# Layer 1 edges: kv tiles in two steps, variances on ScalarE, one message product

## Chip, cores and metric

The kernel runs on one core of a Trainium2 chip, as one launch. The metric is the device time of an execution in microseconds (us). Five engines work side by side, each through its own queue in order: TensorE (PE, with its weight loads PEld), VectorE (DVE), ScalarE (ACT), GpSimd (POOL) and SyncE (SP).

## The reference

Two layers of a graph network over 3125 nodes with 256 features and 50000 edges, all in float32. Each layer adds a message-passing part, a mixing part and a feed-forward part to the node rows. The change lies in layer 1, where the first two are:

```python
h_fwd, h_rev = h @ W_forward.T, h @ W_reverse.T               # 3125 x 64 each
messages = h_fwd[src] * direction[:, 0:1] + h_rev[src] * direction[:, 1:2]
scores = leaky_relu(einsum('ef,hf->eh', messages, attn), 0.2)  # 4 heads
exp_scores = exp(scores - scores.max(axis=0))
norm = exp_scores / (segment_sum(exp_scores, dst)[dst] + 1e-10)
out_gnn = [segment_sum(messages * norm[:, hd:hd+1], dst) for hd in range(4)]

q, k, v = split(x @ Wqkv.T)                                    # 8 heads of 64
k, v = inst_norm_lastdim(k), inst_norm_lastdim(v)              # (t - mean) / sqrt(var + 1e-5)
out_mix = einsum('nhd,hde->nhe', q, einsum('nhd,nhe->hde', k, v)) / n @ Wout.T + bout
```

The edges come sorted by target node (`dst`). What is called Galerkin in the kernel is the second block.

## The kernel before

The nodes stand in 25 tiles of 128 rows (NT = 25, P = 128). The edges stand in 391 columns of 128 (NJ = 391), one edge per partition, and are taken in 50 groups (SPANS): 4 columns, then 48 groups of 8, then 3. Group i adds into a block of 64 nodes.

`layer1_mix` runs over the groups as a pipeline of three stages; the queues of TensorE, VectorE and ScalarE hold the work in exactly the order in which the loop writes it (a manual schedule). In turn i:

- `fetch` and `request`: POOL issues one indirect DMA (`gather`, L71) per column, 128 rows of 136 floats from the table `tab1` into `g`: both products h_fwd and h_rev of the source node, each with its four scores (W = 68 = 64 + 4). Eight gathers of group i+3 are issued in each turn, in portions of 2, 2, 1, 2 and the rest, each portion behind the latest named VectorE operation. `g` has four buffers.
- `messages(i)`, VectorE: the two directions are copied into PSUM (L1652), two products (L1653 and L1654), their sum (L1655), leaky ReLU on the scores (L1657), maximum over the columns (L1662); TensorE turns the maximum (L1664).
- `weigh(i-1)`, VectorE: weights into PSUM (L1702), messages times the weights of four heads (L1703, 128x2048).
- `maximum(i)`, VectorE: running maximum (L1671 to L1673); TensorE spreads it over the partitions (L1677).
- `products(i-1)`, TensorE: one matmul pair per column, one-hot targets against weighted messages (L1709).
- `add(i-2)`: VectorE rescales and adds into `acc` (L1717, L1718); ScalarE copies (L1719, L1721).
- `ones_of(i)`, VectorE: the one-hot matrix `hot` (L1695).
- `exponents(i)`: ScalarE copies the spread maximum out of PSUM (L1682, `top_b`), VectorE subtracts it (L1683), ScalarE takes two exponentials (L1685, L1687).
- then one step of `galerkin`, in three turns out of four up to turn 34 and in every turn after it.

`galerkin` is a generator; each `next` does one step. Its first step makes the weights `wkv`, with each head's mean taken out, so that a key or value has mean zero and its variance is the mean of squares. Then come 26 steps, one per kv tile and one to finish: the step of tile t first ends tile t-1 (sum of its squares L1797, variance L1798, product of the two variances L1800, root on ScalarE L1801, reciprocal L1803, scaling L1804, four matmuls into `pdots` L1807), and then makes tile t (eight matmuls through `token_matmul`, L276; two copies on ScalarE L1817; one square of the whole tile L1819). After the tiles come ten steps that form the product matrix and add its result to x (L1848, L1862, L1864, L1855). The exponentials and the root are in different activation tables, so ScalarE loads a table between them (shown at L1685 and L1801).

Of the kernel before, what the change touches and what calls it, by code (L numbers as in the profile page):

```python
# [9 lines left out]
F32 = mybir.dt.float32  # L10
# [3 lines left out]
AF = mybir.ActivationFunctionType  # L14
OP = mybir.AluOpType
AX = mybir.AxisListType
# [6 lines left out]
P = 128  # L23
NT = 25
# [41 lines left out]
LN_EPS = 1e-5  # L66
# [64 lines left out]
class Kernel:  # L131
# [1462 lines left out]
    def layer1_mix(self, acc):  # L1594
        nc, tc, a = self.nc, self.tc, self.a
        W, HD = 68, 64
        with ExitStack() as m:
            big = m.enter_context(tc.tile_pool(name="l1", bufs=1))
            wk = m.enter_context(tc.tile_pool(name="l1w", bufs=2))
            gp = m.enter_context(tc.tile_pool(name="l1g", bufs=3))  # L1600
            ps_a = m.enter_context(tc.tile_pool(name="l1pa", bufs=2, space=PSUM))
# [5 lines left out]
            xT, tab1 = self.xT, self.tab1  # L1607
# [13 lines left out]
            sides = own[:, 2 * P + 64:2 * P + 64 + 2 * GROUP].rearrange("p (j i) -> p j i", i=2)  # L1621
# [11 lines left out]
            def fetch(i):  # L1633
                j0, n = SPANS[i]
                g = gp.tile([128, GROUP, 2 * W], F32, name="g1", bufs=4)
                wanted.extend((g[:, k, :], self.t_src[:, j0 + k:j0 + k + 1]) for k in range(n))
                return g

            def request(count, behind=None):

                for out, index in wanted[:count]:
                    ins = gather(nc, out, tab1[:], index)
                    if behind is not None:
                        self.after(ins, behind.ins.name, "turns with the groups")
                        behind = None
                del wanted[:count]

            def messages(i, g):

                j0, n = SPANS[i]  # L1650
                o = gp.tile([128, GROUP, W], F32, name="msg1")
                nc.vector.tensor_copy(sides[:, :n, :], self.t_dir[:, j0:j0 + n, :])  # L1652
                nc.vector.tensor_mul(o[:, :n, :], g[:, :n, :W], sides[:, :n, 0:1].to_broadcast([128, n, W]))  # L1653
                nc.vector.tensor_mul(g[:, :n, W:], g[:, :n, W:], sides[:, :n, 1:2].to_broadcast([128, n, W]))  # L1654
                nc.vector.tensor_add(o[:, :n, :], o[:, :n, :], g[:, :n, W:])  # L1655
                s = gp.tile([128, GROUP, 4], F32, name="score1")
                nc.vector.scalar_tensor_tensor(s[:, :n, :], o[:, :n, HD:], 0.2, o[:, :n, HD:],  # L1657
                                               op0=OP.mult, op1=OP.max)
                if j0 + n == NJ:
                    nc.vector.tensor_scalar(s[:, n - 1, :], s[:, n - 1, :], late, None, op0=OP.add)  # L1660
                mx = gp.tile([128, 4], F32, name="mx1")
                self.latest = nc.vector.tensor_reduce(mx, s[:, :n, :].rearrange("p j h -> p h j"), AX.X, OP.max)  # L1662
                pt = ps_s.tile([4, 128], F32, name="psm")
                nc.tensor.transpose(pt, mx, self.ident)  # L1664
                return o, s, pt
# [24 lines left out]
            def ones_of(i):  # L1690

                j0, n = SPANS[i]
                hot = gp.tile([128, GROUP, P], F32, name="hot")
                iota = own[:, i % 2 * P:i % 2 * P + P]
                self.latest = nc.vector.scalar_tensor_tensor(  # L1695
                    hot[:, :n, :], self.t_dst[:, j0:j0 + n, None].to_broadcast([128, n, P]),
                    float(HALF * (1 - i)), iota[:, None, :].to_broadcast([128, n, P]),
                    op0=OP.add, op1=OP.is_equal)
                return hot

            def weigh(n, o, v):
                nc.vector.tensor_copy(weight[:, :n, :], v[:, :n, :, HD])  # L1702
                self.latest = nc.vector.tensor_mul(v[:, :n, :, :HD], o[:, :n, None, :HD].to_broadcast([128, n, 4, HD]),  # L1703
                                     weight[:, :n, :, None].to_broadcast([128, n, 4, HD]))

            def products(n, v, hot):
                pw = ps_w.tile([P, 4, HD + 1], F32, name="pw")
                for k in range(n):
                    nc.tensor.matmul(pw.rearrange("p h c -> p (h c)"), hot[:, k, :],  # L1709
                                     v[:, k, :, :].rearrange("p h c -> p (h c)"), start=(k == 0), stop=(k == n - 1))  # L1710
                return pw
# [13 lines left out]
            with tc.manual_schedule(engines={ET.PE, ET.DVE, ET.Activation}):  # L1725
                todo = self.galerkin(big, wk, ps_a, ps_c, xT, own[:, 2 * P + 96:2 * P + 104])
                S = len(SPANS)
                ahead = [fetch(i) for i in range(3)]
                request(len(wanted))
                msg, exps, summed = {}, {}, {}  # L1730
                for i in range(S + 2):
                    if i + 3 < S:
                        ahead.append(fetch(i + 3))
                    if i < S:
                        n = SPANS[i][1]
                        o, s, pt = messages(i, ahead[i])
                        request(2, self.latest)
                    if 0 <= i - 1 < S:
                        weigh(SPANS[i - 1][1], msg[i - 1][0], exps[i - 1][2])
                        request(2, self.latest)  # L1740
                    if i < S:
                        pb = maximum(pt)
                    if 0 <= i - 1 < S:
                        summed[i - 1] = products(SPANS[i - 1][1], exps[i - 1][2], msg[i - 1][1])
                    if 0 <= i - 2 < S:
                        add(i - 2, *exps[i - 2][:2], summed[i - 2])
                        request(1, self.latest)
                    if i < S:
                        msg[i] = o, ones_of(i)
                        request(2, self.latest)  # L1750
                        exps[i] = exponents(n, s, pb)
                    if i % 4 != 3 or i > 34:
                        next(todo, None)
                    request(len(wanted), self.latest)
                last = exps[S - 1][0]
                for _ in todo:
                    pass
# [10 lines left out]
    def galerkin(self, big, wk, ps_a, ps_c, xT, scales=None):  # L1768
# [3 lines left out]
        nc, a = self.nc, self.a  # L1772
        wkv = big.tile([128, 2, 1024], F32, name="wkv")
# [18 lines left out]
        kvs = {}  # L1792
        for t in range(NT + 1):
            if t > 0:
                kv, sq = kvs.pop(t - 1)
                var = wk.tile([P, 16], F32, name="kv_var")
                nc.vector.tensor_reduce(var, sq, AX.X, OP.add)  # L1797
                nc.vector.tensor_scalar(var, var, 1.0 / 64, LN_EPS, op0=OP.mult, op1=OP.add)  # L1798
                both = wk.tile([P, 8], F32, name="kv_both")
                nc.vector.tensor_mul(both, var[:, 0:8], var[:, 8:16])  # L1800
                nc.scalar.activation(both, both, AF.Sqrt)  # L1801
                inverse = both if scales is None else scales
                nc.vector.reciprocal(inverse, both)  # L1803
                nc.vector.tensor_mul(kv[:, 8:, :], kv[:, 8:, :], inverse[:, :, None].to_broadcast([P, 8, 64]))  # L1804
                for hp in range(4):
                    p = held(t - 1)
                    nc.tensor.matmul(pc[:, hp, :],  # L1807
                                     kv[:p, 8 + 2 * hp:10 + 2 * hp, :].rearrange("p a b -> p (a b)"),
                                     kv[:p, 2 * hp:2 * hp + 2, :].rearrange("p a b -> p (a b)"),
                                     start=(t == 1 and hp == 0), stop=(t == NT and hp == 3),  # L1810
                                     skip_group_check=True)
            if t < NT:
                kv = wk.tile([P, 16, 64], F32, name="kv")
                for i in range(2):
                    pk = ps_a.tile([P, 512], F32, name="ln_pt")
                    self.token_matmul(pk, xT, t, wkv[:, :, 512 * i:512 * i + 512])
                    nc.scalar.copy(kv[:, 8 * i:8 * i + 8, :].rearrange("p a b -> p (a b)"), pk)  # L1817
                sq = wk.tile([P, 16, 64], F32, name="kv_sq", bufs=1)
                nc.scalar.activation(sq, kv, AF.Square)  # L1819
                kvs[t] = kv, sq  # L1820
            yield
        dots = big.tile([128, 4, 128], F32, name="dots")
        nc.vector.memset(dots, 0.0)
        for s in (slice(0, 64), slice(64, 128)):
# [19 lines left out]
        g = big.tile([128, 2, D], F32, name="gm")  # L1844
# [795 lines left out]
```

## Time and profile before

| what | value |
|---|---|
| median of 3 runs | 2501.61 us (2496.76 to 2501.92) |
| the profiled execution, its time | 2496.96 us |
| its span | 2495.2 us |
| busy over the span: PE, DVE, ACT, POOL | 82%, 59%, 33%, 63% |
| first gather to last matmul of the edge stage | 1463.7 to about 2009 us |
| L1703 (`weigh`), full groups | 2.29 us each |
| L1797 (sum of squares) | 25 x 1.21 us |
| L1819 (squares) | 25 x 1.06 us |
| reciprocal L1803 waiting for the root L1801 | 16.4 us in 25 times |

A line of the timeline gives the start in us, the length in us, the engine, the line of the kernel, the operation, the tile written and the tile read, and shapes as partitions x elements; brackets hold the idle time of the engine just before and what ended it. A line of the table by stage gives, for each stretch, the busy us of each engine with the number of instructions, then the mean granted TensorE clock (1 is full), the DMA share and GB/s.

### The profile page before, as it was taken

To read this page: it belongs to the slowest core of one execution; us is meant where nothing else is said; L and a number is where in the kernel's file an instruction comes from. 1 tells how busy PE (TensorE), PEld (TensorE's weight loads), DVE (VectorE), ACT (ScalarE), POOL (GpSimd) and SP (SyncE) were. 2 spreads that over 40 slices of the span, in tenths; PEclk is the share of its full clock that TensorE was granted. 3 is DMA by queue.
4 is the path that set the end of the run, shared out by engine and by line. 5 is a ranking of instruction groups with operands and counts; after the bars stand their busy time and mean duration, and the time that the engine had idled before them with its cause. 6 is when DMAs were issued, how large, how long until landed. Compare 5 with 4: busy or idle time off the path is not lost.

```text
span 2495.2 us, 27313 instructions
## 1 busy us (share of the span) xinstructions
PE 2052.0 (82%) x8239; PEld 1450.5 (58%) x8239; DVE 1465.5 (59%) x3870; ACT 829.8 (33%) x1804; POOL 1565.4 (63%) x1931
## 2 busy tenths in 40 slices
PE   1666799899879989999999647777778779999955
PEld 0433355445555678888888535545556566667644
DVE  6888858986724793221212448888887872223346
ACT  1453144564412113333333324444430042222314
POOL 5888888885000816766666247777776427777743
PEclk9986799999959999999999869999989859999977
DMA  8612539113000225666666332222222112113242
GB/s 269 217 63 102 219 134 324 68 62 111 7 34 5 102 77 164 201 193 200 198 191 187 116 99 55 56 55 56 55 62 46 38 27 38 28 21 80 57 126 78
DMA packets 191721, 263.31 MB, mean 106 GB/s; under 512 B 57234, under 2 KB 152071, under 8 KB 191563
## 3 DMA queue, kind: packets, MB, share of 16 engines
q1 hardware_dynamic: 137551, 211.02, 25.5%
q0 software_dynamic: 48864, 45.64, 8.8%
q10 hardware_dynamic: 5148, 4.80, 0.7%
q8 instruction: 67, 1.10, 0.2%
q14 instruction: 91, 0.75, 0.1%
HBM read 180.80 MB, written 80.55 MB: 105 GB/s over the span
## 4 chain that ended last, share of the span: by engine, by line
PE 59%; DVE 23%; ACT 5%; DMA 4%; POOL 4%; issue 4%; ACTq 0%; DVEq 0%; SPq 0%; POOLq 0%
PE pb L1163 9%; PE pc L1175 8%; PE pb L594 7%; PE fpy L1958 7%; PE fph L1942 7%; DVE v L1703 3%; PE pc L594 3%; PE pw L1709 2%; PE pb L967 2%; PE pc L980 2%; POOL adj L78 2%; PE pb L638 2%; POOL g L71 1%; PE pc L1439 1%; DVE msg L1653 1%
## 5 line engine op out<-in xcount | busy, mean ns | idle before, releaser
L71 POOL DMA_INDIRECT g<-tab,t_src x391 | 378.3, 968 | 197.4 <-issue 153.2
L78 POOL DMA_INDIRECT adj<-ch_sum,ch_place x391 | 415.3, 1062 | 91.0 <-issue 56.5
L78 POOL DMA_INDIRECT sorted<-src,pos x256 | 245.1, 958 | 141.6 <-DVE pos L1462 62.1
L71 POOL DMA_INDIRECT G<-tabg,g_src x256 | 257.9, 1008 | 78.0 <-DMA G<-tabg,g_src 35.7
L1163 PE MATMUL pb<-xs,w 128*128 128x256 f32 x1024 | 226.4, 379 | 0.8 <-ACT h L1165 0.8
L1175 PE MATMUL pc<-w,h 128*128 128x256 f32 x1024 | 226.1, 379 | 0.0
L1709 PE MATMUL pw<-v,hot 128*128 128x260 f32 x782 | 219.5, 442 | 0.0
L1163 PEld LDWEIGHTS pb<-xs,w 128*128 128x128 f32 x1024 | 194.4, 190 | 27.8 <-ACT h L1165 1.0
L594 PE MATMUL pb<-adj,sup 128*128 128x448 f32 (+1 forms) x484 | 196.5, 551 | 14.3 <-DVE r_tot L1309 13.6
L1175 PEld LDWEIGHTS pc<-w,h 128*128 128x128 f32 x1024 | 192.2, 190 | 24.9
L1165 ACT ACTIVATE h<-pb,b 128x256 f32<-128x256 f32 x256 | 121.2, 473 | 253.6 <-issue 168.1
L1709 PEld LDWEIGHTS pw<-v,hot 128*128 128x128 f32 x782 | 169.1, 222 | 31.3
L1958 PE MATMUL fpy<-fw,fh 128*128 128x256 f32 (+1 forms) x800 | 177.7, 379 | 0.0
L1942 PE MATMUL fph<-xT,fw 128*128 128x512 f32 (+2 forms) x448 | 175.2, 545 | 0.0
L1958 PEld LDWEIGHTS fpy<-fw,fh 128*128 128x128 f32 (+1 forms) x800 | 149.6, 187 | 31.8 <-issue 8.2
L78 POOL DMA_INDIRECT slots<-rows,abi x50 | 54.5, 1090 | 164.6 <-DVE which L1085 154.6
L1421 ACT ACTIVATE s_z<-s_y,s_val 128x128 f16<-128x128 f16 x256 | 112.4, 486 | 121.0 <-issue 108.2
L594 PEld LDWEIGHTS pb<-adj,sup 128*128 128x128 f32 x484 | 90.3, 194 | 91.6 <-issue 85.5
L1133 DVE COPY xs<-pa 128x512 f32<-128x512 f32 x32 | 22.1, 691 | 206.6 <-PE pa L1132 206.6
L1944 ACT ACTIVATE fh<-fph,cols 128x512 f32<-128x512 f32 (+2 forms) x112 | 70.3, 632 | 216.2 <-PE fph L1942 216.2
L1942 PEld LDWEIGHTS fph<-xT,fw 128*128 128x128 f32 x448 | 85.7, 192 | 76.7 <-issue 55.8
L1178 DVE SCALAR_TENSOR_TENSOR yo<-pc,own,bg 128x256 f32<-128x256 f32 x64 | 31.0, 484 | 147.0 <-PE pc L1175 147.0
(575 smaller groups left out, 3820.9 us busy)
## 6 DMA issues: line engine op xcount, KB each, us to landing
adj<-zero SPq DMA_DIRECT2D x25, 1600.0 KB
w<-in_L_ffn_W1p_dram SPq DMA_DIRECT2D x32, 1024.0 KB
w<-in_L_ffn_W2p_dram SPq DMA_DIRECT2D x32, 1024.0 KB
adj<-adj SPq DMA_DIRECT2D x24, 896.0 KB
adj<-adj SPq DMA_DIRECT2D x24, 704.0 KB
slots<-empty SPq DMA_DIRECT2D x1, 8448.0 KB
srow<-slots SPq DMA_DIRECT2D x32, 264.0 KB
adj<-ch_sum,ch_place POOLq DMA_INDIRECT x391
```

What stands on the lines that cost most here:

```text
L71: return nc.gpsimd.indirect_dma_start(out=out, out_offset=None, in_=table, in_offset=bass.IndirectOffsetOnAxis(ap=idx, axis=0))
L78: return nc.gpsimd.indirect_dma_start(out=table, out_offset=bass.IndirectOffsetOnAxis(ap=idx, axis=0), in_=rows, in_offset=None, **kw)
L594: nc.tensor.matmul(pm[:, :w], sup[:, b, k * 128:(k + 1) * 128], mats[b, h][:, c0 - PARTS[h][0]:c0 - PARTS[h][0] + w], start=(b == b0), sto ...
L1163: nc.tensor.matmul(ph, w1[:, k, f * 128:(f + 1) * 128], xs[:, k, :], start=(k == 0), stop=(k == 1))
L1165: ins = nc.scalar.activation(h[:, f, :], ph, AF.Gelu, bias=b1[:, f:f + 1])
L1175: nc.tensor.matmul(py, h[:, f, i * 128:(i + 1) * 128], w2[:, f, :], start=(f == 0), stop=(f == FC - 1))
L1421: nc.scalar.activation(z[:, i, k, :], y, AF.Relu, bias=val[:, k, s], scale=val[:, 2 + k, s])
L1703: self.latest = nc.vector.tensor_mul(v[:, :n, :, :HD], o[:, :n, None, :HD].to_broadcast([128, n, 4, HD]), weight[:, :n, :, None].to_broadc ...
L1709: nc.tensor.matmul(pw.rearrange("p h c -> p (h c)"), hot[:, k, :], v[:, k, :, :].rearrange("p h c -> p (h c)"), start=(k == 0), stop=(k == ...
L1942: nc.tensor.matmul(ph[:, :m], w1[:, k, f * 128:(f + 1) * 128], xT[:, k, t0 * P:t0 * P + m], start=(k == 0), stop=(k == 1))
L1944: note(nc.scalar.activation(hs[:, f, :m], ph[:, :m], AF.Gelu, bias=self.col("L1_ffn_b1", ei * FC + f)), m / 512.0)
L1958: nc.tensor.matmul(py[:p], hs[:, f, i * P:i * P + p], w2[:, f, :], start=(f == 0), stop=(f == FC - 1))
```

## The change

Three things are edited.

1. `messages`: the two products become one operation over `g` in place, with the two directions broadcast over the two halves; the sum reads both halves of `g`.
2. `galerkin`: the variances come from ScalarE. Instead of one square of 128x1024 and a sum on VectorE there are 16 squares of 128x64, each with `accum_out` (scale 0.125, so that the sum of squares is divided by 64). A tile's work is cut into two steps: the first ends the variance of tile t-1 up to the root and makes tile t; the second takes the reciprocal, scales and multiplies into `pdots`. With the first step and the last ten there are now 62.
3. `layer1_mix`: `advance(half)` takes the steps. It is called twice in each turn, between `products` and `add` and after `exponents`, and keeps the number of steps done in proportion to the number of halves, so that the 62 steps are spread over the first 46 turns.

```diff
-                nc.vector.tensor_mul(o[:, :n, :], g[:, :n, :W], sides[:, :n, 0:1].to_broadcast([128, n, W]))
-                nc.vector.tensor_mul(g[:, :n, W:], g[:, :n, W:], sides[:, :n, 1:2].to_broadcast([128, n, W]))
-                nc.vector.tensor_add(o[:, :n, :], o[:, :n, :], g[:, :n, W:])
+                both = g[:, :n, :].rearrange("p j (i w) -> p j i w", i=2)
+                nc.vector.tensor_mul(both, both, sides[:, :n, :, None].to_broadcast([128, n, 2, W]))
+                nc.vector.tensor_add(o[:, :n, :], g[:, :n, :W], g[:, :n, W:])
...
+                done, every = 0, 2 * NT + 12
+
+                def advance(half):
+
+                    nonlocal done
+                    while done * 2 * (S - 4) < half * every:
+                        next(todo, None)
+                        done += 1
...
                         summed[i - 1] = products(SPANS[i - 1][1], exps[i - 1][2], msg[i - 1][1])
+                    advance(2 * i + 1)
                     if 0 <= i - 2 < S:
                         add(i - 2, *exps[i - 2][:2], summed[i - 2])
...
                         exps[i] = exponents(n, s, pb)
-                    if i % 4 != 3 or i > 34:
-                        next(todo, None)
+                    advance(2 * i + 2)
                     request(len(wanted), self.latest)
...
         for t in range(NT + 1):
             if t > 0:
-                kv, sq = kvs.pop(t - 1)
-                var = wk.tile([P, 16], F32, name="kv_var")
-                nc.vector.tensor_reduce(var, sq, AX.X, OP.add)
-                nc.vector.tensor_scalar(var, var, 1.0 / 64, LN_EPS, op0=OP.mult, op1=OP.add)
+                kv, var = kvs.pop(t - 1)
+                nc.vector.tensor_scalar(var, var, LN_EPS, None, op0=OP.add)
                 both = wk.tile([P, 8], F32, name="kv_both")
                 nc.vector.tensor_mul(both, var[:, 0:8], var[:, 8:16])
                 nc.scalar.activation(both, both, AF.Sqrt)
+            if t < NT:
+                nxt = wk.tile([P, 16, 64], F32, name="kv")
+                for i in range(2):
+                    pk = ps_a.tile([P, 512], F32, name="ln_pt")
+                    self.token_matmul(pk, xT, t, wkv[:, :, 512 * i:512 * i + 512])
+                    nc.scalar.copy(nxt[:, 8 * i:8 * i + 8, :].rearrange("p a b -> p (a b)"), pk)
+                sq = wk.tile([P, 64], F32, name="kv_sq", bufs=1)
+                var = wk.tile([P, 16], F32, name="kv_var")
+                for h in range(16):
+                    nc.scalar.activation(sq, nxt[:, h, :], AF.Square, scale=0.125, accum_out=var[:, h:h + 1])
+                kvs[t] = nxt, var
+            yield
+            if t > 0:
                 inverse = both if scales is None else scales
                 nc.vector.reciprocal(inverse, both)
...
                                      skip_group_check=True)
-            if t < NT:
-                kv = wk.tile([P, 16, 64], F32, name="kv")
...
-                sq = wk.tile([P, 16, 64], F32, name="kv_sq", bufs=1)
-                nc.scalar.activation(sq, kv, AF.Square)
-                kvs[t] = kv, sq
-            yield
+                yield
```

More of the change, by code (lines that the diff above doesn't have):

```diff
@@ L1811, in galerkin @@
                                      skip_group_check=True)
-            if t < NT:
-                kv = wk.tile([P, 16, 64], F32, name="kv")
[L1814 to L1817, printed above, removed]
-                sq = wk.tile([P, 16, 64], F32, name="kv_sq", bufs=1)
-                nc.scalar.activation(sq, kv, AF.Square)
-                kvs[t] = kv, sq
-            yield
+                yield
         dots = big.tile([128, 4, 128], F32, name="dots")
```

## The prediction

> **What bounds the kernel now.** I read the page first, then the busy time by stage, then the timeline of the edge stage. The edges of layer 1 run from 1464 to 2010 us. While they carry the kv tiles (to about 1850 us) the stages look like this:
>
> ```profile
> core 0: us, PE busy (x) PEld busy (x) DVE busy (x) ACT busy (x) POOL busy (x), PEclk, DMA share, GB/s
> 1500.00:1600.00 100.00, 75.39 (x294) 51.15 (x295) 87.14 (x174) 44.38 (x90) 76.23 (x79) 0.95 0.25 56
> 1600.00:1700.00 100.00, 75.79 (x288) 51.91 (x287) 89.29 (x177) 40.80 (x86) 75.92 (x80) 0.91 0.25 55
> ```
>
> VectorE is busy 87 to 89%, ScalarE 41 to 44%. POOL's 79 gathers in 100 us, each with 0.30 us of issue before it, also fill their queue (8 x 1.27 = 10.2 us per group). VectorE sets the pace: the starts of `weigh` (L1703) at 1626.45, 1637.97, 1645.90, 1657.10 and 1668.62 are 11.5, 7.9, 11.2 and 11.5 us apart. The 7.9 is the one group in four without a kv step. Four groups take 42.6 us (1602.88 to 1645.90 to 1688.07, halved), so three take 31.95.
>
> Why ScalarE costs nothing now is seen in the timeline of one kv group:
>
> ```profile
> 1613.18 3.60 PE L276 MATMUL ln_pt<-wkv,xT 128*128 128x512 f32 x8
> ...
> 1616.82 0.58 ACT L1817 COPY kv<-ln_pt 128x512 f32<-128x512 f32 x1 [1.13 <-PE ln_pt L276]
> ...
> 1617.43 1.06 ACT L1819 ACTIVATE kv_sq<-kv 128x1024 f32<-128x1024 f32 x1
> ...
> 1618.60 0.37 ACT L1721 COPY acc<-pw 64x260 f32<-64x260 f32 x1
> ...
> 1618.99 0.17 ACT L1682 COPY top_b<-psm 128x8 f32<-128x8 f32 x1
> ...
> 1619.42 0.18 DVE L1683 TENSOR_TENSOR score<-score,top_b 128x32 f32<-128x32 f32 x1
> ```
>
> TensorE makes the kv tile, ScalarE copies it, squares it in 1.06 us, and only then reaches L1682, the copy of the maximum. VectorE needs that copy for L1683, one short subtraction that stands in its queue ahead of the whole next group. Here L1682 ends at 1619.16 and `hot` (L1695, from 1618.29 for 1.21 us) at 1619.50: L1683 waits for nothing, with 0.3 us to spare. **That margin is what the change spends.**
>
> **Part 1, one message product.** L1653 and L1654 (721 and 714 ns, 128x544) become one of 128x1088. Rows at 544 and 2048 elements (721 and 2287 ns) give 1.04 ns an element, so 1.29 us; bounds 0.72 (no dearer than one) and 1.43 (both). With the shorter start interval a group's VectorE work gains 0.06 us; by the bounds it gains 0.6 or loses 0.1, at most 30 us over 50 groups, if VectorE sets the pace.
>
> **Part 2, the variances.** Off VectorE goes L1797 (25 x 1.21 = 30.2 us), and the wait of the reciprocal for the root (16.4 us in all) disappears by the two steps. On ScalarE one square of 1.06 us becomes 16 squares of 64 elements, each with its own accumulator. The nearest row is L825:
>
> ```profile
> 210.62 0.38 ACT L825 ACTIVATE sq<-pb 128x256 f32<-128x256 f32 x1 [0.79 <-PE pb L823]
> 210.90 0.19 ACT L825 ACTIVATION_READ_ACCUMULATOR sq<-pb 128x1 f32 x1
> 211.12 0.38 ACT L825 ACTIVATE sq<-pb 128x256 f32<-128x256 f32 x1
> ```
>
> Each accumulator costs a second instruction, and the pair repeats every 0.50 us. The square itself shrinks from 0.383 to 0.255 us (ACTIVATEs of 48 and 96 elements take 243 and 282 ns), so a pair takes 0.375 and a tile **16 x 0.375 = 6.0 us**. Bounds: 0.29 a pair if the read cost nothing (0.255 + 0.03), 0.45 if nothing overlapped (0.255 + 0.195); 4.6 to 7.2 us. All write one `kv_sq`, so each waits for the one before; dependent pieces of ScalarE follow after 0.03 us (L1817 to L1819), which is in the price.
>
> **Part 3, where the steps stand.** Step k is taken at the first half with h > 1.484 k. Tile t's heavy step A (variance end, root, eight matmuls, two copies, 16 squares) is step 2t, near h = 3t; its light step B (reciprocal, scaling, `pdots`) is step 2t+1, near h = 3t+2. So three groups carry two tiles:
> - X: A in the first half, between `products` and `add`.
> - Y: B in the first half, A in the second.
> - Z: B in the second half, but Y's squares stand on ScalarE before its L1682.
>
> The listing of ScalarE's instructions in the changed kernel shows the same: two groups running have 16 squares between their `grown` and the next L1682, the third has none. Before, A came after the exponents, so TensorE worked on the tile while VectorE made the next group's messages. In X it starts only after this group's products.
>
> **X, walked along the wait.** From L1652 to the end of L1673: 5.98 us on VectorE in the group at 1634.83, now 5.92. Transposition and start of products 0.2. Products (L1709) 3.77. The kv matmuls 3.5 (3.60 less overlap). The second copy 0.6. Squares 6.0. `unit`, `acc` and L1682 0.6. L1683 0.2. Sum **20.8 us**. VectorE's own work in X is about 8.4; the other 12 it stands at L1683, with the next group's messages behind it, and POOL's gathers wait for their turns behind those.
>
> **Y and Z.** Y has only VectorE work: 5.92, B's two operations 0.95, L1717 and L1718 0.92, `hot` 1.14, L1683 0.18, the variance's two 0.4: 9.5. Y's products start 6.1 after its own start; 3.77 to 9.9, `pdots` to 10.85, kv matmuls to 14.35, copy to 14.95, squares to 20.95, L1682 to 21.55, L1683 to 21.75, B of Z to **22.7 us** for Y and Z together.
>
> Three groups: 20.8 + 22.7 = 43.5 us. **The clock** adds to this. A product after a quiet TensorE is slow:
>
> ```profile
> 1687.97 0.27 PE L1664 MATMUL psm<-ident,mx 128*4 128x128 f32 x1 [1.01 <-DVE mx L1662]
> 1690.88 0.36 PE L1677 MATMUL psm<-ident,top 4*128 4x4 f32 x2 [2.64 <-DVE top L1672]
> 1691.16 6.56 PE L1709 MATMUL pw<-v,hot 128*128 128x260 f32 x16
> ...
> 1703.05 3.77 PE L1709 MATMUL pw<-v,hot 128*128 128x260 f32 x16
> ```
>
> The slow ones of three neighbouring cases took 6.49, 5.46 and 6.56 us, 6.2 on average. In X the products come after the same two waits, in Y after TensorE has stood through X's squares (over 6 us): both are slow, and both on the path, 2 x 2.4 = 4.8 us. Three groups: 48.3 us.
>
> The Trainium skill (TensorE: Matmul & The Clock Gate, Part 1: The HAM clock gate) halves the clock only after an idle window of about 3.4 us and gives it back after as much work. The trace goes slow after 1.01 and 2.64 us with a 0.27 us transposition between. By the rule X would stay fast and Y lose about 1.7 us, an estimate, for 2663 us.
>
> **The sum.** 25 tiles are 12.5 rounds of three: 12.5 x (48.3 - 31.95) = **+205 us**. The other pieces I take at nothing. The last ten galerkin steps fall on eight groups, not on eleven; TensorE sets the pace there (11.4 us a group) and does the same matmuls, so what each group gains is gone in the number; from the two sides -8 to +8. Table loads (1.28 us, L1685 and L1801) are as many as before at most: the root's runs while ScalarE waits for the matmuls, the exponent's under 2.7 us of the next messages; without that cover 25 x 1.28 = 32 us. The 391 gathers keep number, queue and order; POOL's 30 us per round hide under 48. SP's load of Wout only moves. The profiled execution took 2496.96 us (span 2495.2), 4.65 under the median of 2501.61; the sum is 2497 + 205 = **2702 us**, and that offset, as wide as the spread of the runs, is left out.
>
> **The rivals.**
> - Clock stays full: 12.5 x (43.5 - 31.95) = +144, 2641 us. For it: X's products follow `pdots` by some 4 us only. Against: the 6.56 row.
> - Accumulators dearer: at 0.45 a pair 1.2 us more per tile, +30, 2732; at 0.5, as L825 with its 256 elements, 2 us more per tile, +50, 2752.
> - Accumulators cheap: 0.29 a pair, -1.4 per tile, -35: 2667, or 2606 with the clock full.
> - It ends faster: ScalarE has 4.9 us more per tile, two tiles in 30.6 us of a POOL-paced round, so its share rises from 44% to about 76%. If the squares fell into ScalarE's idle time and L1682 did not queue behind them, VectorE would need 3 x 7.9 + 2 x 1.35 = 26.4 us per round, POOL's 30.6 (three times 10.2) would bind, and 12.5 x (30.6 - 31.95) = -17 gives 2480. It decides at 0.3 us, the margin of L1682 above; against it, the order of ScalarE's queue.
> - The change does not do what it says, since the even spreading loses to the place of A: part of my forecast. Even with squares at their old 1.06 us, X would need 20.8 - 4.9 = 15.9 against 8.4.
>
> **How the numbers follow.** Forecast (slow products, 0.375 a pair) 55%; full clock 22%; dearer accumulators 12%; cheap ones 6%; the faster case 4%; a balance near nothing 1%. The range reaches from 2606, cheap squares at full clock, to 2765 (0.5 a pair, plus 8 of the tail and 5 of the runs' spread). A measurement tells 0.2% from no change. Faster 0.04, same 0.01, slower 0.95.
>
> **What would show it.** Right: L1683 waiting for ScalarE some 25 times, about 15 us in X and 5 to 7 in Z; group starts 23, 9.5 and 16 us apart; a granted clock well under 0.9 between 1500 and 2050 us; POOL idle behind VectorE. Wrong: no wait at L1683, the 16 squares under 3 us, or POOL without idle time.

## The result and the profile after

The changed kernel takes 2697.57 us (median of 4 runs, 2696.01 to 2698.29) against 2499.19 us for the kernel before in the same comparison: ratio 1.0799, 95% interval 1.0771 to 1.0827, 198 us slower. The forecast was 2702 us. The profiled execution has a span of 2696.6 us.

First the stages of the edge part, busy us by engine, then the granted clock:

```profile
core 0: us, PE busy (x) PEld busy (x) DVE busy (x) ACT busy (x) POOL busy (x), PEclk, DMA share, GB/s
1500.00:1600.00 100.00, 53.96 (x179) 37.13 (x178) 50.38 (x101) 48.43 (x200) 56.47 (x60) 0.76 0.19 42
1600.00:1700.00 100.00, 54.42 (x178) 37.55 (x178) 51.03 (x103) 47.60 (x196) 46.00 (x48) 0.74 0.15 34
1700.00:1800.00 100.00, 55.13 (x179) 37.84 (x179) 54.26 (x108) 43.97 (x182) 47.87 (x50) 0.74 0.15 35
```

VectorE fell from 87-89% to 50-54%, POOL from 76% to 46-56%, the clock from 0.91-0.95 to 0.74-0.76, and ScalarE, which was given the work, is busy hardly more than before (44-48% against 41-44%). No engine is full: this is a kernel that waits. The list of waits from 1500 to 2000 us says for whom (us in total, times, longest):

```profile
DVE score L1683 <- ACT top_b L1682: 193.9, 21, 15.4
POOL g L71 <- DVE own_bank L1702: 178.3, 20, 14.9
```

Before, L1683 had no wait in the list; now VectorE stands there 194 us of 500, and POOL stands behind VectorE. What ScalarE does in that time is seen in its timeline in X (L1813 is now the copy of the kv tile, L1817 the square):

```profile
1739.40 0.59 ACT L1813 COPY kv<-ln_pt 128x512 f32<-128x512 f32 x1 [1.13 <-PE ln_pt L276]
1739.88 0.26 ACT L1817 ACTIVATE kv_sq<-kv 128x64 f32<-128x64 f32 x1
1740.04 0.19 ACT L1817 ACTIVATION_READ_ACCUMULATOR kv_sq<-kv 128x1 f32 x1
1740.26 0.26 ACT L1817 ACTIVATE kv_sq<-kv 128x64 f32<-128x64 f32 x1
...
1745.75 0.19 ACT L1817 ACTIVATION_READ_ACCUMULATOR kv_sq<-kv 128x1 f32 x1
...
1746.42 0.16 ACT L1682 COPY top_b<-psm 128x8 f32<-128x8 f32 x1
```

A pair of square and read repeats every 0.38 us, 16 of them fill 1739.88 to 1745.94, and only then comes L1682. VectorE's timeline shows the other side, first Z, then X:

```profile
1717.20 1.21 DVE L1695 SCALAR_TENSOR_TENSOR hot<-t_dst,own_bank 128x1024 f32<-128x1024 f32 x1
1722.97 0.19 DVE L1683 TENSOR_TENSOR score<-score,top_b 128x32 f32<-128x32 f32 x1 [4.57 <-ACT top_b L1682]
...
1731.19 1.22 DVE L1695 SCALAR_TENSOR_TENSOR hot<-t_dst,own_bank 128x1024 f32<-128x1024 f32 x1
1746.61 0.19 DVE L1683 TENSOR_TENSOR score<-score,top_b 128x32 f32<-128x32 f32 x1 [14.20 <-ACT top_b L1682]
```

The turns begin (L1652) at 1698.94 (Y), 1708.24 (Z), 1724.04 (X) and 1746.72 (the next Y): 9.3, 15.8 and 22.7 us, a round of 47.8 us. The kernel before needed 31.95 us for three groups; 12.5 rounds make 12.5 x (47.8 - 31.95) = 198 us. That this equals the whole loss is chance: it takes one round for all of them. The starts of the groups (L1652, counted from 0) tell where the loss arises. Group 38, the first behind the kv tiles, starts so before and after:

```profile
1878.92 0.18 DVE L1652 COPY own_bank<-t_dir 128x16 f32<-128x16 f32 x1
```

```profile
2065.73 0.18 DVE L1652 COPY own_bank<-t_dir 128x16 f32<-128x16 f32 x1
...
2108.33 0.19 DVE L1683 TENSOR_TENSOR score<-score,top_b 128x32 f32<-128x32 f32 x1 [9.11 <-ACT top_b L1682]
```

So 187 us are lost by the end of the kv tiles, though the kernel before has by then done three of the last ten steps of `galerkin` as well. At group 45 it is 203 (1964.21 against 2167.70), and it stays there to the last group: another 17 us arise while the changed kernel does all ten steps, on eight groups instead of ten and in the middle of turns too. One part of it is seen in the last line: VectorE waits 9.1 us for ScalarE, where the kernel before waits 0.2 us in all from 1850 to 2010 us; the rest was not taken apart. (The two profiled executions are 201 us apart, the medians 198.)

### The profile page after: what moved, and what is told of

Its sections match the earlier page's. It is cut to its first block, busy times and chain, and to the rows that moved or that the text cites. A ratio compares the mean times of both kernels' runs of the same rounds, so it can differ in the third digit from the quotient of the medians.

```text
span 2696.6 us, 27977 instructions
## 1 busy us (share of the span) xinstructions
PE 2105.5 (78%) x8239; PEld 1488.8 (55%) x8239; DVE 1428.9 (53%) x3795; ACT 940.8 (35%) x2579; POOL 1564.8 (58%) x1931
## 4 chain that ended last, share of the span: by engine, by line
PE 61%; DVE 19%; ACT 7%; POOL 6%; DMA 4%; issue 3%; SPq 0%; DVEq 0%; ACTq 0%; POOLq 0%
PE pb L1163 8%; PE pc L1175 8%; PE pb L594 7%; PE fpy L1968 6%; PE fph L1952 6%; PE pw L1709 6%; ACT kv_sq L1817 4%; POOL adj L78 3%; PE ln_pt L276 3%; DVE v L1703 3%; PE pc L594 2%; PE pb L967 2%; PE pc L980 2%; DVE g L1654 2%; PE pb L638 1%
## 5 line engine op out<-in xcount | busy, mean ns | idle before, releaser
L1709 PE MATMUL pw<-v,hot 128*128 128x260 f32 x782 | 255.7, 497 | 0.0
L1709 PEld LDWEIGHTS pw<-v,hot 128*128 128x128 f32 x782 | 194.6, 255 | 42.0
L1683 DVE TENSOR_TENSOR score<-score,top_b 128x32 f32<-128x32 f32 (+2 forms) x50 | 9.3, 186 | 225.6 <-ACT top_b L1682 225.6
```

## The experiments

Each is compared with the kernel before, run beside it on the same chip (medians 2498.8 and 2499.07 us). The changed kernel's 2697.57 us stands beside 2499.19.

**One message product alone** (the kernel before with the first part of the diff). This and the next two try the three parts one at a time.

```diff
...
+                nc.vector.tensor_mul(both, both, sides[:, :n, :, None].to_broadcast([128, n, 2, W]))
+                nc.vector.tensor_add(o[:, :n, :], g[:, :n, :W], g[:, :n, W:])
```

> The kernel before with the single message product alone. The forecast's part 1 (1.29 us against 0.72 + 0.71) gives 0.06 us a group where VectorE sets the pace: 0 to 3 us faster, 2494 to 2500 us. If the one product were the cause of the loss, it would be some 200 us slower.

Measured 2490.44 us, ratio 0.9971 (0.9959 to 0.9983): 8 us faster. The operation takes 1.29 us, as reckoned. The last kv matmul starts at nearly the same time as before (1848.3 against 1848.9 us), so in the kv stage nothing is gained; the last addition of the edge stage (L1718) starts at 2002.2 instead of 2009.7. Part of that is VectorE's waits for TensorE, which shrink behind the kv stage (L1718 for the products 3.3 to 0.4 us, L1840 4.2 to 2.5, L1671 22.0 to 20.8); the rest was not taken apart. This part does no harm.

**The variances on ScalarE alone**, in the old place at the turn's end, with one step a tile.

```diff
-                sq = wk.tile([P, 16, 64], F32, name="kv_sq", bufs=1)
-                nc.scalar.activation(sq, kv, AF.Square)
...
+                for h in range(16):
+                    nc.scalar.activation(sq, kv[:, h, :], AF.Square, scale=0.125, accum_out=var[:, h:h + 1])
```

> The kernel before with the variances on ScalarE alone: 16 squares in the old place, at the turn's end, and one step per tile. Theory (the squares stand ahead of L1682): a kv group loses 4.9 us of squares less the 0.3 us of margin, and 1.2 us of VectorE's sum of squares goes out but is replaced by a longer wait for the root: about +4.6 us in 25 groups, +115 us, 2590 to 2640 us. Rival (ScalarE has room, only the new places of the steps cost): 30 us less work on VectorE, 2470 to 2490 us.

Measured 2634.3 us, ratio 1.054 (1.0523 to 1.0558), +135. The list of waits from 1500 to 1850 us:

```profile
DVE score L1683 <- ACT top_b L1682: 80.9, 18, 5.0
DVE own_bank L1801 <- ACT kv_both L1799: 38.0, 17, 2.7
```

80.9 us in 18 waits is 4.5 us each, where 4.6 was reckoned: the squares beyond the margin. The wait for the root grew from 0.66 to 2.2 us, because the sum on VectorE, during which the table was loaded before, is gone. Per kv group that is 4.5 + 1.6 - 1.2 = 4.9 us, 122 in 25; the other 13 were not taken apart. Taking 30 us of work off VectorE cost more than it saved even where the steps stood well.

**The places alone**: two steps and `advance` as in the change, with one square, the sum on VectorE and two products.

```diff
-                    if i % 4 != 3 or i > 34:
-                        next(todo, None)
+                    advance(2 * i + 1)
...
+                    advance(2 * i + 2)
```

> The change's two steps and its even spreading, with the old variances (one square of 1.06 us, sum on VectorE) and the two products. Theory (step A in the first half waits for this turn's products): X 15.9 us and 2.4 us for a slow product, Y and Z set by VectorE, 19.6 us; a round of 35.5 to 37.9 us against 31.95, +45 to +75 us, 2540 to 2575 us. Rival (only the 16 squares cost): no change or a few us faster, 2480 to 2500 us.

Measured 2582.96 us, ratio 1.034 (1.0323 to 1.0357), +84. Turns begin at 1689.55, 1699.73, 1709.69 and 1727.25 us: 10.2, 10.0 and 17.6, a round of 37.7, the upper end of what was reckoned. 12.5 x (37.7 - 31.95) is 72 us; the rest is the last ten steps again: group 38 starts 69 us later than before, group 45 86. So both the squares and the places cost time, each by itself: -8, +135 and +84 add up to 211, against 198 together.

**Late squares**: the changed kernel, with its 400 squares written behind the next exponents: step A only notes the tile, and `squares` makes the 16 squares of each noted tile (at the latest when the next step A begins).

```diff
                         exps[i] = exponents(n, s, pb)
+                    if done > 1:
+                        self.squares()
...
+                self.owed.append((nxt, var))
```

> The changed kernel with the same 400 squares, only put off behind the next exponents, so that they no longer stand ahead of L1682. Theory (order in ScalarE's queue): X falls by 6.0 us to 14.8 and 2.4 for the slow product, Y and Z are set by VectorE at about 19 us; a round of about 36 us against 48.3: 150 us faster than the changed kernel, 2530 to 2570 us. Rival (the amount of ScalarE's work, 6 us a tile wherever it stands): stays near 2697 us.

Measured 2576.53 us, ratio 1.0317 (1.03 to 1.0334), 121 us faster than the changed kernel with the same work. Turns begin at 1690.62, 1699.49, 1711.15 and 1728.25 us: a round of 37.6 where 36 was reckoned. The end of X:

```profile
1690.33 0.16 ACT L1682 COPY top_b<-psm 128x8 f32<-128x8 f32 x1
...
1690.52 0.19 DVE L1683 TENSOR_TENSOR score<-score,top_b 128x32 f32<-128x32 f32 x1 [8.45 <-ACT top_b L1682]
```

The wait in X falls from 14.20 to 8.45 us, and the 4.57 in Z is gone. What is left in X is no square: it is the wait for the kv matmuls, which step A in the first half puts behind this turn's products. The amount of ScalarE's work is therefore not the cause of what the squares cost; their place in the queue is. With the squares late the kernel loses 78 us, about what the places alone lose without any of them (84, or some 76 with the one product).

**The copy on VectorE**: the changed kernel with L1682 moved, so that L1683 needs nothing from ScalarE.

```diff
-                nc.scalar.copy(big2, pb)
+                nc.vector.tensor_copy(big2, pb)
```

> The changed kernel with the copy of the maximum (L1682) on VectorE, so that L1683 waits for nothing on ScalarE. Theory (the whole of the exponents stands behind the squares, L1685 too): the wait moves to L1702, which needs the exponents, and only the 0.9 us by which a table load and an exponential are shorter than the next messages are gained in X and Z: about 20 us faster than the changed kernel, 2665 to 2685 us. Rival (only the copy is badly placed): the loss goes away almost whole, 2500 to 2530 us.

Measured 2653.88 us, ratio 1.0617 (1.0601 to 1.0633), 44 us faster than the changed kernel: twice what was reckoned, far from the rival's 2500 to 2530. The waits of VectorE, 1500 to 1850 us:

```profile
DVE own_bank L1702 <- ACT v L1685: 113.5, 16, 13.7
```

The wait moved to the exponents, as the theory says. Its size was misjudged: the next messages (2.65 us) now run during the wait, so `weigh` starts 2.4 us after the squares. In the changed kernel it started 3.7 us after them in X and 4.8 in Z (1745.94 to 1749.68, 1722.28 to 1727.11). That is 1.3 + 2.4 = 3.7 us a round, 46 in 12.5.

**Stirred**: the changed kernel with matmuls that nobody reads, to keep TensorE busy: two of 512 columns behind L1664, ten behind the kv matmuls of X.

```diff
+                if 1 < done < 2 * NT + 2:
+                    stir(2)
...
+                    if before != done and before % 2 == 0 and 2 <= before < 2 * NT:
+                        stir(10)
```

> The changed kernel with idle matmuls on TensorE, whose result nobody reads: two of 512 columns behind each turned maximum, ten behind the kv matmuls of X. Theory (slow products after a quiet TensorE are 4.8 us of a round of 48): products of 3.8 us everywhere, a round of about 43.5 us, up to 60 us faster than the changed kernel, 2637 to 2660 us. Rival (the products' speed is hidden behind ScalarE's squares): 2690 us or more.

Measured 2655.22 us, ratio 1.0631 (1.0615 to 1.0648), 42 us faster. Products of the changed kernel (X), then those of the stirred one in Z and X, where L1677 and L1709 have become L1685 and L1717:

```profile
1724.06 2.08 PE L1826 MATMUL pdots<-kv 128*128 128x128 f32 x8 [3.60 <-DVE kv L1823]
1727.01 0.37 PE L1664 MATMUL psm<-ident,mx 128*4 128x128 f32 x1 [0.87 <-DVE mx L1662]
1729.92 0.35 PE L1677 MATMUL psm<-ident,top 4*128 4x4 f32 x2 [2.54 <-DVE top L1672]
1730.20 5.73 PE L1709 MATMUL pw<-v,hot 128*128 128x260 f32 x16
```

```profile
1700.20 3.77 PE L1717 MATMUL pw<-v,hot 128*128 128x260 f32 x16
...
1713.27 0.37 PE L1685 MATMUL psm<-ident,top 4*128 4x4 f32 x2
1713.58 4.11 PE L1717 MATMUL pw<-v,hot 128*128 128x260 f32 x16
```

The granted clock rises from 0.74 to 0.91-0.93, the products of this round take 3.77 to 4.11 us instead of 5.73 to 6.38 in X and Y, and the round 44.35 us (1684.13 to 1728.48). A kernel that does more work is faster, since the slow clock stood on the path. It gets 42 of the 60 us: in X the stirring itself runs slowly (3.62 us) and delays L1677.

**Turn's end**, the version that beats both: step A only behind the exponents, step B in the middle of the next turn, evenly over 46 turns; one square and VectorE's sum as before; the one product.

```diff
+                    if half % 2 == 1 and light or half % 2 == 0 and heavy * 2 * (S - 4) < half * (NT + 12):
                         next(todo, None)
+                        heavy += not light
+                        light = not light and 3 <= done + 1 <= 2 * NT + 1 and done % 2 == 0
                         done += 1
```

> The heavy step A only at a turn's end, behind the exponents, the light step B in the middle of the next turn, spread evenly over 46 turns; the variances as in the kernel before (one square, sum on VectorE); the one message product. Theory: L1682 never stands behind more than one 1.06 us square, VectorE needs 7.9 us and in 26 of 34 turns 2.5 us more, 9.8 us on average, so POOL's 10.2 us a group bind: 10 to 20 us faster than before, 2477 to 2490 us. Rival (any spreading in two steps costs, because step A's matmuls stand ahead of the next turn's transposition): not faster than before, 2497 us or more.

Measured 2479.13 us, ratio 0.992 (0.9906 to 0.9933), 20 us faster than before; the one product, which alone brought 8, is part of it. VectorE no longer waits for ScalarE between 1500 and 1850 us. POOL's list of waits in that stretch begins so:

```profile
POOL g L71 <- issue: 55.4, 182, 0.3
POOL g L71 <- DMA g<-tab,t_src: 21.6, 71, 0.3
```

All are the 0.3 us steps from one gather to the next: 79 to 81 gathers in each 100 us, back to back. But the kernel before issues as many there (79, 80 and 79), so not much can be gained in this stretch: group 35 starts 9 us earlier (1839.3 against 1847.9). The other half of the gain comes later. From 1850 to 2000 us POOL's gathers waited for VectorE in the kernel before:

```profile
POOL g L71 <- DVE own_bank L1702: 13.9, 8, 3.4
POOL g L71 <- DVE acc L1718: 7.7, 3, 5.1
```

In turn's end 2.6 us of the first are left and none of the second. The 391 gathers then take 498 us from the first to the last, 1.28 us each, instead of 514: POOL is the bound over nearly the whole edge stage. The last gather starts at 1962.4 instead of 1978.1 us, and the last addition (L1718) at 1992.3 instead of 2009.7.

## Why the prediction was right

- **The wait at L1683** was foretold some 25 times, about 15 us long in X and 5 to 7 in Z; there are 24 in the kv stage, 14.20 and 4.57 us in the rows, so a little shorter than said in Z. The group starts 23, 9.5 and 16 us apart came out as 22.7, 9.3 and 15.8. Late squares and the copy on VectorE show that it is the order of ScalarE's queue, not its load, that makes VectorE wait.
- **The price of the squares**, 16 x 0.375 = 6.0 us, measured 16 x 0.38 (1716.22 to 1722.28 is 6.06). This refutes both rivals on the accumulators (0.29, and 0.45 or 0.5 a pair).
- **The slow products** were put at 2.4 us each in X and Y; 5.73 and 6.38 are 2.0 and 2.6 over 3.77. Stirring shows that at least 42 us of the loss hang on it; the rival of the full clock (2641 us) falls with a granted clock of 0.72 to 0.76.
- **The rule on the clock** that was weighed (the Trainium skill, TensorE: Matmul & The Clock Gate, Part 1: The HAM clock gate), with an idle window of about 3.4 us and an estimate of 2663 us, was taken to leave X fast. X came out slow, but not for the reason given. The prediction had only the two short gaps in X; the trace shows TensorE idle for 3.60 us ahead of `pdots` as well, and the granted clock is 0.99 from 1720 to 1724 us and 0.50 from 1724 to 1730. The 2.8 us of TensorE's work that followed, with gaps of 0.87 and 2.54 us, did not bring it back. So X agrees with the rule, and the estimate fell because this gap was left out. What the rule, read as one unbroken gap, does not explain is the row that the prediction went by (1.01 and 2.64 us, with 0.27 us of work between) and X of the places alone: there `pdots` follows the products at once, the gaps are 1.35 and 2.63 us, and the products take 5.46 us. There the measurement decides.
- **Part 1** was reckoned at 0.06 us a group and at most 3 us alone; alone it brought 8, and not in the stage that was looked at. A term mis-sized by at least 5 us, with little weight beside 198.
- **The faster rival** failed at the point named for it: L1682 came up to 15.4 us later than VectorE needed it. Turn's end comes to the 2479 us that this rival named, but it is no test of it: it leaves the sum of squares on VectorE, and half of its gain arises behind the kv tiles.
- **The nearness of the sum is partly luck.** It had 205 us from the kv tiles and nothing from the rest; the group starts show 187 and 17. The last ten steps were bounded at -8 to +8 us, from eleven groups to eight; they lay on ten before. The same term appears in the other kernels with these places: from group 38 to group 45 the places alone lose 16 us, late squares 14, stirred 17 and the copy on VectorE 17, while the variances alone, with the steps in their old places, lose none (-1). The table loads did stay at nothing: 25 at the root and 26 at L1685, before and after.

## What to carry to other kernels

Idle time of an engine is not room: before work is given to a lightly loaded engine, look for the instruction in its queue that the bounding engine waits for, and count how many us the new work may stand ahead of it (0.3 us here, against 6). Order is cheaper to change than work: the same 16 squares cost 121 us less a few places later. Of a step cut in two, the light half, which only needs something already finished, cost nothing in the middle of a turn here (turn's end); the heavy half belongs behind the last thing that others wait for.

## What the runs showed of the hardware

An accumulator on ScalarE is an instruction of its own (187 ns on average over 400 of them), so 16 squares of 64 columns with accumulators take 6.06 us where one square of 1024 columns takes 1.06. And matmuls without any use made a kernel 42 us faster, by keeping the granted clock at 0.91 to 0.93 instead of 0.74.
